# A two-layer decoder on one core: PSUM tiles of single values, value writes on ScalarE's queue, and another order of expert blocks

## The chip, the core and the metric

The kernel runs on one core of one Trainium2 chip. The metric is the device time of one execution in microseconds (us); lower is better. A core has a TensorE (PE) for matrix products, a VectorE (DVE), a ScalarE (ACT), a GpSimd (POOL) and a SyncE (SP); each runs its own instructions in order and waits for the others by semaphores. DMA transfers are issued from the queues of SP, ACT and POOL. PE writes to PSUM, which has eight banks of 128 partitions x 512 floats; the kernel's tiles lie in the on-chip SBUF, its inputs and scratch arrays in DRAM.

## The reference, cut to what matters

The function is a decoder of two layers over x (4 sequences of 512 rows, 256 wide) with a context of 4 x 1601 rows. Each step adds to x and normalizes:

```python
x = _layernorm(x + _L0_attn_ref(x, ...))            # an inner gradient step per token
x = _layernorm(x + _L0_xattn_ref(x, ctx, ctx, fside, ...))
x = _layernorm(x + _L0_ffn_ref(x, ...))             # 8 experts, the best 2 per row
x = _layernorm(x + _L1_attn_ref(x, ...))            # 16 heads, causal
x = _layernorm(x + _L1_xattn_ref(x, ctx, ctx, mask, ...))   # 16 heads, rotary
x = _layernorm(x + _L1_ffn_ref(x, ...))
```

Two parts of it bear on the change. The experts, of which each row needs only two:

```python
y = vmap(_expert_ffn)(xf, Wi, bi, Wg, bg, Wo, bo, gamma, beta)
# h = gelu(xf @ Wi + bi) * sigmoid(xf @ Wg + bg); r = xf + h @ Wo + bo; normalized, * g + b
out = einsum('te,eth->th', c, y)                    # c: the two weights of each row
```

and the values of the last cross attention, `V = value @ Wv.T` for each context. They don't depend on x, and so can be computed at any time before they are used.

## The kernel before

All products are in float32. The work goes through four stages: the first attention (to about 240 us), the first cross attention with the choice of experts (to 529 us), the experts (547 to 1001 us), and the second layer with both attentions and the last feed-forward part (1001 us to the end). Within a stage, the order of the instructions on each engine is that of the Python code (`manual_schedule`): nothing is moved by a scheduler.

**PSUM.** From the second stage on, `psum_stage` (L48) gives three pairs of banks, tag "wide" (`wide()`, L55), and two single banks, tag "bank" (`bank()`, L58), each used in turn. A tile that comes round again waits until the last reader of its former contents is done.

**Early values.** At the end of the second stage, `value(b, k)` (L782) computes the values of the contexts 2 and 3 for one block of 128 context rows: four PE records (two products of 128x256, each seen as two records), and a copy by ScalarE (L791) into an SBUF tile in the layout that the later attention needs. There are 26 of them, in the order 9 of context 2, 13 of context 3, 4 of context 2 (L831). Two successive values share one pair of banks, through the list named `halves`. The first 9 are placed between the parts of the last normalization and of the routing (`tail()`, L834 to L841); the other 17 follow `blocks_left` (L551), whose VectorE work gives the tables of the dynamic expert blocks. After the values (2, 8), (3, 12) and (2, 12), SP writes what is finished to the DRAM arrays `vd` (L793, L795, L797; 1291.5, 1865.5 and 574 KB). They are read again in the second layer's cross attention. Meanwhile POOL scatters the rows of x to the experts' array `xs` (L546).

**SP's queue at the start of the third stage.** After the writes to `vd`, SP issues the eight weight loads of the second layer (L79; the first is qkvQ), four small vectors (L92, L85), the rows of the first two expert blocks (`rows_of`, L922), and two eWo loads (L407). The weights take memory that the values' tiles had.

**Expert blocks.** `run(blocks, work)` (L1110) processes a list of blocks of 256 rows. A block of kind "f" (first) has the first 256 rows of one expert and one set of weights; a block of kind "m" (more) has two halves of 128 rows, each with a dynamically chosen expert and weights of its own. An expert's weights are eWi and eWg (1028 KB each) and eWo (1408 KB). Those of an "f" block are loaded by SP (`load_expert`, L399), those of an "m" block by POOL with indirect DMAs, and so are the rows (L922 and L928). Iteration i does, in this order: `first_half(i)` (products with eWi and eWg, gelu and sigmoid on ScalarE, the product of both on VectorE, L977; it also issues the loads of eWi and eWg of block i+1), `turned(i+1)` (transposes of the rows, L939), `second_half(i-1)` (products with eWo, VectorE's sum from L997 on, normalization, the write to `ys` by SP, L1012; for an "m" block, PE's second half waits for VectorE's first sum), `rows_of(i+2)`, the next eWo loads (three are held ahead), and one step of the side work `attention_first` (L1019). The steps of the side work go by position in the list: 0 to 2 load constants and tables, 3 to 6 fill rows of `qd` and `ksd`, 7 to 10 fill `kcd` (1601 KB each, DRAM to DRAM), 11 clears tiles on POOL, 12 to 15 each load a piece of the mask by SP (L1068), which VectorE turns into an additive row (L1072).

The order of the blocks is written out by hand as a string (L1143), 8 "f" and 11 "m".

Of the kernel before, what the change touches and what calls it, by code (L numbers as in the profile page):

```python
# [18 lines left out]
B, S, D = 4, 512, 256  # L19
S2 = 1601  # L20
NT = S // P
NKT = (S2 + P - 1) // P
# [12 lines left out]
def kn_of(kt):  # L35
    return P if kt < NKT - 1 else KLAST
# [3 lines left out]
def decoder(ctx: ExitStack, tc: tile.TileContext, a: dict, out: bass.AP):  # L40
    nc = tc.nc
# [13 lines left out]
    def wide():  # L55
        return psum["A"].tile([P, 2, 512], F32, tag="wide", name="wide")

    def bank():  # L58
        return psum["B"].tile([P, 512], F32, tag="bank", name="bank")
# [15 lines left out]
    def weight(pool, name):  # L75

        src = a[name]
        t = pool.tile([P, 2, src.shape[1]], F32, tag=name, name=name)
        nc.sync.dma_start(t, src.rearrange("(c p) n -> p c n", p=P))  # L79
        return t  # L80
# [117 lines left out]
    def mm(ps, terms):  # L198

        n = len(terms)  # L200
        for i, (l, r) in enumerate(terms):
            nc.tensor.matmul(ps, l, r, start=(i == 0), stop=(i == n - 1))  # L202
# [12 lines left out]
    with (  # L215
# [15 lines left out]
        ps = wide()  # L231
# [4 lines left out]
        ps = bank()  # L236
# [387 lines left out]
    VROW = NH * VW + HD - 1  # L624
    vd = {b: tc.dram_tile((P, NKT * VROW), F32, name=f"vd{b}") for b in (2, 3)}


    with tc.tile_pool(name="p2", bufs=2) as p2, ExitStack() as ordered:
# [7 lines left out]
        ps = wide()  # L636
# [3 lines left out]
        ps = bank()  # L640
# [3 lines left out]
        ps = wide()  # L644
# [3 lines left out]
        ps = bank()  # L648
# [115 lines left out]


        xaV = weight(p2, "xaV")
        values, places, halves = [], {}, []

        def rows_of_values(first):

# [10 lines left out]

        def value(b, k):  # L782
            kn = kn_of(k)
            if not halves or len(halves) == 2:
                halves[:] = [wide()]
            else:
                halves.append(halves[0])
            ps = halves[0][:, len(halves) - 1, :D]
            mm(ps[:kn], [(ctxTs[b][:, c, k * P : k * P + kn], xaV[:, c, :]) for c in range(2)])
            dst = places[b, k][:kn, : NH * VW].rearrange("p (h r) -> p h r", r=VW)  # L790
            nc.scalar.copy(dst[:, :, :HD], ps[:kn].rearrange("p (h r) -> p h r", r=HD))  # L791
            if (b, k) == (2, 8):
                nc.sync.dma_start(vd[2][:, : 9 * VROW], big_of(2, 0, 9))  # L793
            if (b, k) == (3, NKT - 1):
                nc.sync.dma_start(vd[3], big_of(3, 0, NKT))  # L795
            if (b, k) == (2, NKT - 1):
                nc.sync.dma_start(vd[2][:, 9 * VROW :], big_of(2, 9, NKT))  # L797

        def big_of(b, k0, k1):
            first = places[b, k0]  # L800
            return bass.AP(first.tensor, first.offset, [first.ap[0], [1, (k1 - k0) * VROW]])
# [29 lines left out]
        order = [(2, k) for k in range(9)] + [(3, k) for k in range(NKT)]  # L831
        order += [(2, k) for k in range(9, NKT)]
        values = [lambda b=b, k=k: value(b, k) for b, k in order]
        for n in (3, 0, 0, 0, 0, 0, 6, 0, 0, 0, 0, 0):  # L834
            if len(values) < len(order):
# [5 lines left out]
            values = values[n:]  # L841
# [52 lines left out]
    with tc.tile_pool(name="p3", bufs=2) as p3, ExitStack() as ordered:  # L894
# [245 lines left out]
                next(work, None)  # L1140
            second_half(blocks[-1], None, outs)

        order = "ffmfmfmmfmfmmfmfmm" + "m" * 1  # L1143
        counts = {"f": iter(range(E)), "m": iter(range(NDYN // 2))}
        blocks = [({"f": "first", "m": "more"}[k], next(counts[k])) for k in order]
        def beside():
# [25 lines left out]
    with ExitStack() as s4:  # L1172
# [148 lines left out]
        def context(b, keys, values, here=None):  # L1321
# [20 lines left out]
            for i in sorted({*keys, *values}):  # L1342
                if here is None:
                    src = lambda n=len(stream): chunk(n)
                    stream.append((b, i))
                else:
                    src = lambda i=i: here[2 * i : 2 * i + 2]
                eng = nc.gpsimd if here is None else nc.vector
                if i in keys:
                    items += [lambda s=src, i=i, c=c: key(s, i, c, eng) for c in range(2)]  # L1350
                if i in values:
                    items += [lambda s=src, k=k: value(s, k) for k in range(4 * i, min(4 * i + 4, NKT))]
# [650 lines left out]
```

## Time and profile before

| what | value |
|---|---|
| median of 3 runs | 2409.47 us (2403.08 to 2413.41) |
| the profiled execution, its own time | 2402.61 us |
| its span, first to last instruction | 2400.8 us |
| PE busy | 2275.6 us (95%) |
| DVE, ACT, POOL busy | 1239.0, 1064.2, 360.0 us (52%, 44%, 15%) |
| DMA moved | 244.14 MB, mean 102 GB/s |

By stretches of the span, as the windows of the trace give them (busy us; share of the DMA engines):

| stretch, us | length | PE | DVE | ACT | granted clock | DMA |
|---|---|---|---|---|---|---|
| 487 to 507 | 20 | 15.84 | 9.25 | 4.62 | 0.83 | 0.14 |
| 507 to 529 | 22 | 17.89 | 7.03 | 6.71 | 1.00 | 0.47 |
| 529 to 547 | 18 | 0.19 | 0.00 | 0.00 | 0.55 | 0.85 |
| 547 to 593 | 46 | 41.99 | 6.79 | 18.98 | 0.84 | 0.45 |
| 593 to 1001 | 408 | 382.45 | 157.88 | 207.26 | 0.98 | 0.76 |
| 1001 to 2401 | 1400 | 1368.33 | 885.56 | 738.44 | 0.98 | 0.15 |

A line of the timeline has the start and the length of a group of instructions in us, the engine (PEld is PE's weight load, SPq a DMA issue in SP's queue), the source line, the operation, the tile written and the tile read, the shape, the number of instructions, and in brackets the idle time of the engine just before, with what ended it. The granted clock is the share of full speed that PE's clock was allowed.

### The profile page before, as it was taken

To read this page: it belongs to the slowest core of one execution; us is meant where nothing else is said; L and a number is where in the kernel's file an instruction comes from. 1 tells how busy PE (TensorE), PEld (TensorE's weight loads), DVE (VectorE), ACT (ScalarE), POOL (GpSimd) and SP (SyncE) were. 2 spreads that over 40 slices of the span, in tenths; PEclk is the share of its full clock that TensorE was granted. 3 is DMA by queue.
4 is the path that set the end of the run, shared out by engine and by line. 5 is a ranking of instruction groups with operands and counts; after the bars stand their busy time and mean duration, and the time that the engine had idled before them with its cause. 6 is when DMAs were issued, how large, how long until landed. Compare 5 with 4: busy or idle time off the path is not lost.

```text
span 2400.8 us, 36163 instructions
## 1 busy us (share of the span) xinstructions
PE 2275.6 (95%) x14448; PEld 1289.9 (54%) x14448; DVE 1239.0 (52%) x2928; ACT 1064.2 (44%) x2103; POOL 360.0 (15%) x373
## 2 busy tenths in 40 slices
PE   7899999968999999889999999999999999999998
PEld 4767577757898988643333334333333333333266
DVE  1433234431333334356666667666766776677234
ACT  1111122213554545324555553655656566566730
POOL 1010001130122223225230010120122010000000
PEclk9999999988999999989999998999999999999999
DMA  8400311135887867341210210111110010100000
GB/s 304 173 0 1 132 55 46 45 137 178 321 333 308 338 258 300 132 147 50 67 49 27 77 64 1 37 33 59 56 58 28 25 60 15 54 11 20 30 10 27
DMA packets 77100, 244.14 MB, mean 102 GB/s; under 512 B 11640, under 2 KB 34686, under 8 KB 64638
## 3 DMA queue, kind: packets, MB, share of 16 engines
q1 hardware_dynamic: 60126, 137.41, 16.7%
q0 software_dynamic: 13632, 89.32, 9.7%
q10 hardware_dynamic: 3168, 15.03, 1.8%
q8 instruction: 116, 1.90, 0.3%
q14 instruction: 58, 0.48, 0.1%
HBM read 196.12 MB, written 56.77 MB: 105 GB/s over the span
## 4 chain that ended last, share of the span: by engine, by line
PE 50%; DVE 1%; ACT 1%; issue 0%; DVEq 0%; ACTq 0%
PE s L1458 23%; PE po L1485 12%; PE one L202 11%; PE s L202 2%; PE s L1468 1%; PE one L1443 1%; PE one L1506 1%; ACT x L171 0%; ACT ex L1472 0%; DVE pm L1415 0%; DVE one L1417 0%; PE one L1527 0%; PE one L1625 0%; PE one L1548 0%; DVE nb L166 0%
## 5 line engine op out<-in xcount | busy, mean ns | idle before, releaser
L1472 ACT ACTIVATE ex<-s 128x512 f32<-128x512 f32 (+1 forms) x1062 | 578.2, 594 | 458.2 <-PE s L1458 222.8
L1415 DVE TENSOR_REDUCE pm<-one 128x1 f32<-128x512 f32 x768 | 492.8, 685 | 159.5 <-PE s L1458 104.0
L1458 PE MATMUL s<-q,kc 32*128 32x512 f32 x1612 | 527.6, 638 | 0.8 <-ACT ex L1472 0.8
L202 PE MATMUL one<-kc,qt 32*128 32x512 f32 (+1 forms) x2048 | 482.5, 562 | 0.3 <-DVE pm L1415 0.3
L1458 PEld LDWEIGHTS s<-q,kc 32*128 32x128 f32 x1612 | 165.9, 179 | 202.5 <-issue 170.0
L1485 PE MATMUL po<-ex,v 128*32 128x256 f32 (+3 forms) x2688 | 250.9, 442 | 0.3 <-ACT ot L1498 0.3
L1417 DVE CUSTOM_DVE_ANT_0 one<-one,c_diagq 128x512 f32<-128x512 f32 x256 | 171.8, 716 | 76.0 <-PE one L202 65.1
L1485 PEld LDWEIGHTS po<-ex,v 128*32 128x32 f32 (+1 forms) x2688 | 54.1, 108 | 252.4 <-issue 244.9
L1458 PE MATMUL s<-q,ks 32*128 32x512 f32 x512 | 180.0, 650 | 5.3 <-ACT ex L1472 4.9
L202 PEld LDWEIGHTS one<-kc,qt 32*128 32x128 f32 x2048 | 164.2, 188 | 11.8 <-DVE pm L1415 7.8
L202 PE MATMUL bank<-eWo,g 128*128 128x256 f32 x608 | 141.9, 390 | 13.6 <-DVE rb L997 10.7
L202 PE MATMUL one<-ks,qt 32*128 32x512 f32 x512 | 149.7, 662 | 0.6 <-DVE pm L1417 0.6
L202 PE MATMUL wide<-xbT,eWi 128*128 128x128 f32 (+1 forms) x960 | 142.9, 310 | 4.0 <-DVE xbT L943 4.0
L202 PEld LDWEIGHTS wide<-xbT,eWi 128*128 128x128 f32 x960 | 132.9, 196 | 13.4 <-issue 3.4
L977 DVE TENSOR_TENSOR g<-g,sg 128x1024 f32<-128x1024 f32 x38 | 46.3, 1223 | 178.5 <-ACT sg L975 178.5
L202 PE MATMUL wide<-xbT,eWg 128*128 128x128 f32 (+1 forms) x960 | 137.0, 303 | 0.0
L202 PEld LDWEIGHTS bank<-eWo,g 128*128 128x128 f32 x608 | 116.4, 196 | 33.5 <-DVE rb L997 14.8
L1298 POOL TENSOR_TENSOR raw<-raw,c_cos 128x512 f32<-128x512 f32 (+1 forms) x32 | 35.0, 1094 | 654.8 <-DVE swp L1297 554.8
L202 PEld LDWEIGHTS wide<-xbT,eWg 128*128 128x128 f32 x960 | 128.1, 191 | 6.6
L1458 PEld LDWEIGHTS s<-q,ks 32*128 32x128 f32 x512 | 53.9, 185 | 83.3 <-issue 61.7
L202 PE MATMUL wide<-ctxT,q 128*128 128x512 f32 (+1 forms) x256 | 91.3, 510 | 0.8 <-DVE q L669 0.8
L975 ACT ACTIVATE g<-wide,eWi 128x128 f32<-128x128 f32 (+1 forms) x240 | 72.6, 415 | 27.0 <-PE wide L202 26.8
(326 smaller groups left out, 2943.0 us busy)
## 6 DMA issues: line engine op xcount, KB each, us to landing
xs<-zero SPq DMA_DIRECT2D x32, 512.0 KB
kc<-kcd SPq DMA_DIRECT2D x16, 800.5 KB
eWo<-in_eWo SPq DMA_DIRECT2D x8, 1408.0 KB
eWi<-in_eWi SPq DMA_DIRECT2D x8, 1028.0 KB
eWg<-in_eWg SPq DMA_DIRECT2D x8, 1028.0 KB
qt<-qd SPq DMA_DIRECT2D x32, 256.0 KB
ctxT<-in_ctxT SPq DMA_DIRECT2D x4, 1601.0 KB
kcd<-in_c_rowkc ACTq DMA_DIRECT2D x4, 1601.0 KB
```

Of the source, the lines that this page charges most:

```text
L202: nc.tensor.matmul(ps, l, r, start=(i == 0), stop=(i == n - 1))
L975: nc.scalar.activation(dst[:, k, :], pv[:, k, :], func, bias=bias)
L977: nc.vector.tensor_tensor(part, part, dst, ALU.mult)
L1298: eng.tensor_tensor(raw[:, :n], raw[:, :n], cos[:, :n], ALU.mult)
L1415: nc.vector.tensor_reduce(pm[:, t, j, c : c + 1], ps, AX.X, ALU.max)
L1417: nc.vector.tensor_tensor_reduce(out=ps, in0=ps, in1=diagq[:, 384 - t * P : 896 - t * P], scale=1.0, scalar=LOWEST, op0=ALU.add, op1=ALU.m ...
L1443: nc.tensor.transpose(pt[:, t * P : (t + 1) * P], ng.rearrange("p j r -> p (j r)"), ident)
L1458: nc.tensor.matmul(ps[:kn], kt[rows, k * P : k * P + kn], q2[rows, :], start=True, stop=cross)
L1468: nc.tensor.matmul(ps[:, k * P : (k + 1) * P], later_[:, :P], later_[:, P:], start=False, stop=True)
L1472: nc.scalar.activation(ex[:kn, h, :], ps[:kn], AF.Exp)
L1485: nc.tensor.matmul(state["po"][j * 32 : j * 32 + 32, q0:q1], (vals if cross else vself)[b % 2][:kn, k, c0 : c0 + 32], ex[:kn, j % 2, q0:q1 ...
L1506: nc.tensor.transpose(pt[:, t * P : (t + 1) * P], ot[:, t * P : (t + 1) * P], ident)
```

## The change

It has three parts. First, a value no longer shares a PSUM pair with its neighbour: of each three successive values, two take a single bank, and the third takes half of a pair of its own. Second, the three writes to `vd` are issued from ScalarE's queue instead of SP's, at the same places of the code. Third, the string that gives the order of the expert blocks is another one; the numbers of both kinds stay as they are. With positions counted from 0, "m" and "f" change places at 5 and 6, at 10 and 11, and at 15 and 16.

```diff
-        values, places, halves = [], {}, []
+        values, places, turns = [], {}, [0]
...
         def value(b, k):
             kn = kn_of(k)
-            if not halves or len(halves) == 2:
-                halves[:] = [wide()]
-            else:
-                halves.append(halves[0])
-            ps = halves[0][:, len(halves) - 1, :D]
+            turns[0] += 1
+            ps = wide()[:, 0, :D] if turns[0] % 3 == 0 else bank()[:, :D]
             mm(ps[:kn], [(ctxTs[b][:, c, k * P : k * P + kn], xaV[:, c, :]) for c in range(2)])
             dst = places[b, k][:kn, : NH * VW].rearrange("p (h r) -> p h r", r=VW)
             nc.scalar.copy(dst[:, :, :HD], ps[:kn].rearrange("p (h r) -> p h r", r=HD))
             if (b, k) == (2, 8):
-                nc.sync.dma_start(vd[2][:, : 9 * VROW], big_of(2, 0, 9))
+                nc.scalar.dma_start(vd[2][:, : 9 * VROW], big_of(2, 0, 9))
             if (b, k) == (3, NKT - 1):
-                nc.sync.dma_start(vd[3], big_of(3, 0, NKT))
+                nc.scalar.dma_start(vd[3], big_of(3, 0, NKT))
             if (b, k) == (2, NKT - 1):
-                nc.sync.dma_start(vd[2][:, 9 * VROW :], big_of(2, 9, NKT))
+                nc.scalar.dma_start(vd[2][:, 9 * VROW :], big_of(2, 9, NKT))
...
-        order = "ffmfmfmmfmfmmfmfmm" + "m" * 1
+        order = "ffmfmmfmfmmfmfmmf" + "m" * 2
```

## The prediction

> **What bounds the kernel.** The page gives PE 95% of the span. Its chain of waits carries 50% of the span by PE, but it starts at 1126 us, in the second layer's attention, where the change touches nothing; from 1001 us on PE is busy 1368 of 1400 us, so that part only shifts. What is gained or lost must therefore come from PE's own gaps before 1001 us. I read those in the timeline, from 484 to 1003 us. First the values:
>
> ```profile
> 490.25 1.99 PE L202 MATMUL wide<-xaV,ctxT 128*128 128x256 f32 x8 [2.13 <-ACT v L791]
> ...
> 517.74 1.99 PE L202 MATMUL wide<-xaV,ctxT 128*128 128x256 f32 x8 [0.46 <-ACT v L791]
> 518.91 0.37 ACT L791 COPY v<-wide 128x256 f32<-128x256 f32 x1 [1.22 <-PE wide L202]
> 519.77 0.37 ACT L791 COPY v<-wide 128x256 f32<-128x256 f32 x1 [0.49 <-PE wide L202]
> 520.20 1.99 PE L202 MATMUL wide<-xaV,ctxT 128*128 128x256 f32 x8 [0.46 <-ACT v L791]
> ...
> 529.03 0.32 SPq L797 DMA_DIRECT2D vd<-v  x1
> 531.87 0.38 SPq L79 DMA_DIRECT2D qkvQ<-in_qkvQ  x1
> ...
> 543.54 1.07 SPq L922 DMA_DIRECT2D xb<-xs  x2
> 546.81 1.08 PE L939 MATMUL bank<-ident,xb 128*128 128x128 f32 x4 [18.22 <-DMA xb<-xs]
> ```
>
> The reader is to see two limits. PE stands before every second value until ScalarE has copied the other half of the same pair: the period is 520.20 - 517.74 = 2.46 us for two values, while two copies released by PE stand 519.77 - 518.91 = 0.86 us apart, which is PE's own time for one value. And the 18.22 us gap before the first expert block is a string on SP: the last write of values at 529.03, its landing, the weights' issues from 531.87, the rows of the first blocks at 543.54. Then the expert stage, from the waits of PE between 540 and 980 us and its timeline:
>
> ```profile
> PE bank L939 <- DMA xb<-xs: 24.6, 5, 18.2
> PE bank L202 <- DVE rb L997: 10.5, 10, 3.2
> ...
> 768.01 0.63 PE L939 MATMUL bank<-ident,xb 128*128 128x128 f32 x4 [3.46 <-DMA xb<-xs]
> ...
> 858.00 0.52 DVE L1072 TENSOR_SCALAR mf<-mi 16x401 f32<-16x401 int32 x1 [12.86 <-DMA mi<-in_mask]
> ...
> 862.37 5.17 PE L202 MATMUL bank<-eWo,g 128*128 128x256 f32 x16 [3.02 <-DVE rb L997]
> ```
>
> No wait on eWi or eWg is listed: weights arrive in time. What is left is small: 24.6 - 18.2 = 6.4 us on rows of blocks, two waits of about 3 us on VectorE, which had itself waited for a piece of the mask.
>
> **Part 1: single banks.** No instruction is added; 26 values keep four PE records and one copy each. What goes is the wait inside a pair, since no tile holds two values now. A bank comes round after three values, and its copy is due 2 x 0.86 = 1.72 us after PE left it; a copy needs 0.1 + 0.37 us, and 0.4 more where a DMA issue stands before it on ScalarE, so it is covered. Were that cover gone, each value would wait the difference. In order:
> - Values 1 to 3: the transposes of x start when VectorE has x (491.35) instead of at 492.08: **0.7 us**, and the routing chain behind them shifts by it.
> - Values 4 to 9: they start at 497.6 instead of 498.29. The copies at 500.40 and 502.11 show 1.7 us per value there (granted clock 0.50 from 498 to 503 us). Two at 1.7 and four at 0.86 end at 504.5; VectorE's carry, ready at 504.8 - 0.7 = 504.1, is covered. The routing matmuls start at 504.5 instead of 507.07: **2.6 us**.
> - Values 10 to 26: the first two take banks that VectorE must read first (L525, L556). L556 stood 2.04 us after the routing matmuls (509.11 - 507.07), so value 11 starts at 506.7; 16 x 0.86 = 13.8 ends at 520.5, instead of 528.6: **8.1 us** in all, the 2.6 among it.
>
> [...] Here the granted clock fell at 497 us though no gap since 487 was over 2.13 us. [...]
>
> **Part 2: writes by ScalarE's queue.** Three issues of about 0.33 us leave SP and become three of about 0.4 us on ScalarE (its c_diagq issue took 0.39). Behind the first two stand copies, and PE behind those; part 1 covers them. The obvious hope is that SP, freed, starts its weights at once. I don't count it: the order of instructions of the changed kernel still has the qkvQ load wait for the DMA lanes that the values' writes are on, and before it waited 531.87 - 529.03 = 2.84 us for the last of them. POOL's first eWo load waits the same way (13.5 us for vd). So the string stays: last copy, last write, landing, weights (14.94 us from 531.87 to PE's 546.81), and only its start moves. The last write, issued at 521.0 instead of 529.03, comes closer to the one before it (1865 KB at the 478 GB/s of the windows from 525 to 528 us is 3.9 us): that one, issued at 517.6, has its data through at 522.3, the last (574 KB, 1.4 us) at 523.7, and qkvQ follows 0.65 us later at 524.35. Gain of parts 1 and 2 together: 531.87 - 524.35 = **7.5 us**. Bounds: 8.5 us if the two writes don't queue and the clock doesn't fall; 5 us if three more values run at half clock (3 x 0.85). The scatter of the last rows, on POOL until 519.3 before, moves 2.5 us ahead with L556 and stays covered.
>
> If the write did not hold qkvQ, up to 3.4 us more (524.35 - 521.0) would go; that is in rival C.
>
> **Part 3: order of blocks.** The same 8 whole blocks ("f") and 11 of halves ("m"), three swaps of neighbours: positions 5/6, 10/11, 15/16. The side work (tables, masks), one step per position, keeps its positions. PE's work is the same; only gaps can move.
> - *Weights of pairs.* The pair at 9, 10 stands beside the kcd copies. Before, the pair at 11, 12 stood beside two of the four, and PE ran from 797 to 833 us without a wait on weights. I take 0, bounds 0 and +6: eWg of the first half has 12.3 us from issue to use in a pair (699.1 to 711.4), and eWg landed after 13.5 us (median) in the busiest stretch, 728 to 775.
> - *Rows of whole blocks.* Six "m to f" changes before and after. SP issues the rows about 5.8 us into the block before when an f precedes that, 4.2 us after an m. Landings stood 15.2 to 15.8 us into that block in three cases, 17.9 beside kcd (f at position 10, 3.46 us). For position 11 the row gives 5.8 + 13.7 from issue to landing = 19.5, a wait of 5.2 us. [...]
> - *Mask pieces.* A piece holds VectorE when its steps fall in a fast f block behind an m: before at positions 13 and 15, 3.0 us each, and PE then ran at 5.17 instead of 3.72 us for its 16 (half clock), so 4.5 us each. After: 13 and 16 the same; 15, now an m behind an m, has its sigmoid 0.8 us later but also a reader that waits: between 0 and 4.5, taken as 2.3.
> - *End.* The last eWo half is loaded behind position 17 in both (wait of 2.92 us): 0. The activation-table load of the first block no longer waits for PE; PE ran on through it before: 0.
>
> Sum of part 3: **+2.8 us**, bounds -2 and +13.
>
> **Sum.** -7.5 + 2.8 = -4.7 us. Against the profiled execution 2402.6 - 4.7 = 2397.9 us. Its span is 2400.8; it lies 6.9 us under the median of the three runs and 0.5 us under the fastest of them (2403.1 to 2413.4), so it is an execution at the fast end. The median is what is compared: 2409.5 - 4.7 = **2404.8 us**, said as 2405.
>
> **Rivals.**
> - *B, the order costs more than the values gain.* Around positions 9 and 10 the DMA needs 4.1 MB of weights, some 2.8 MB of eWo and 3.3 MB of kcd traffic in a block of 21.6 us: 470 GB/s, where the busiest slices show 420 to 450. If the backlog passes the 12.3 us of slack, PE waits at both halves of 10 and again on the rows of 11: 6 + 6 + 4.5 of masks + half-clock starts of 1.5 each (3) = 19.5, net +12: 2421. For it: eWg's 13.5 us. Against it: the older pair beside kcd did not wait. It decides once a weight takes more than 12.3 us from issue to landing inside a pair.
> - *C, more is gained:* qkvQ isn't held by the last write (-3.4) and the new order avoids one mask stall and the rows' wait beside kcd (-4.5, -3.5): -7.5 - 11.4 = -18.9: 2391. For it: waits on shared lanes need not be on the last write. Against it: the same memory is written by the weights.
> - *D, the change doesn't do what it says:* VectorE's readers hold the two banks, so that values go on waiting and only the order acts: +2.8: 2412. Against it: only values 10 and 11 have such a reader.
>
> **Numbers.** The forecast 0.58, B 0.19, C 0.16, D 0.07. What a measurement of this kernel can tell from no change is 0.5%, 12 us: below 2397.4 or above 2421.5. The forecast's own range is 2398 to 2413 (its bounds, and about 3 us of spread of medians). Half of B is below 2421; with C's near half the range is 2394 to 2418. Faster by over 0.5%: most of C and the forecast's lower edge, 0.24. Slower by over 0.5%: most of B and a little of D, 0.16. Within: 0.60.
>
> **What would show it.** Values: PE in runs without a wait on L791, copies 0.86 us apart, the last copy near 521. SP: qkvQ near 524.4, PE's first block near 539.3; if qkvQ starts at 521, C is right there. Order: waits on rows at positions 6, 8 and 11 (the last 3 to 5 us), on VectorE at 13, 16 and perhaps 15; any PE wait on eWi or eWg speaks for B. The start of the second layer, 1001 before, should be near 996. Wrong altogether if that shift is there and the end doesn't follow it.

## The result, and the profile after

The changed kernel takes 2398.11 us (median of 20 runs, 2388.19 to 2408.62) against 2404.26 us before (20 runs beside them, 2395.72 to 2413.41). The medians lie 6.15 us apart; the ratio is 0.9966, with a 95% interval from 0.9955 to 0.9977, which is about 8 us less and under the bound of 0.5% (12 us). The forecast of -4.7 us lies close to it. The profiles show that two of its terms were wrong in opposite directions.

The profiled execution of the changed kernel took 2408.62 us and was the slowest of the 20, so its end says nothing against the medians. Its span is 2406.8 us, with PE busy 2285.7 us. Its timeline around the end of the values, with the columns as in the views of before:

```profile
515.87 0.37 ACT L788 COPY v<-wide 128x256 f32<-128x256 f32 x1 [0.49 <-PE wide L202]
516.74 0.37 ACT L788 COPY v<-bank 128x256 f32<-128x256 f32 x1 [0.49 <-issue]
518.51 0.37 ACT L788 COPY v<-bank 128x256 f32<-128x256 f32 x1 [1.40 <-PE wide L202]
520.65 0.37 ACT L788 COPY v<-wide 128x256 f32<-128x256 f32 x1 [1.76 <-PE bank L202]
523.49 0.37 ACT L788 COPY v<-bank 128x256 f32<-128x256 f32 x1 [2.46 <-remote]
...
531.84 0.33 ACTq L794 DMA_DIRECT2D vd<-v  x1
534.71 0.37 SPq L79 DMA_DIRECT2D qkvQ<-in_qkvQ  x1
546.48 1.04 SPq L919 DMA_DIRECT2D xb<-xs  x2
549.66 1.09 PE L936 MATMUL bank<-ident,xb 128*128 128x128 f32 x4 [18.26 <-DMA xb<-xs]
```

Up to 516.74 us the copies stand 0.86 us apart, as the single banks should give. Then ScalarE falters: the next three copies take 6.75 us (516.74 to 523.49) instead of 2.6, and its idle time has another releaser in each line. After that PE waits for ScalarE. So in this execution the values end no earlier than before: qkvQ starts 44.9 us after the first value's start (534.71 - 489.81), and before the change it was 44.8 us (531.87 - 487.09). SP's string behind it is the old one, with a gap of 18.26 us.

The expert stage of the same execution, from its timeline:

```profile
790.63 0.63 PE L936 MATMUL bank<-ident,xb 128*128 128x128 f32 x4 [1.62 <-DMA xb<-xs]
863.39 5.41 PE L202 MATMUL bank<-eWo,g 128*128 128x256 f32 x16 [3.16 <-DVE rb L994]
909.23 3.72 PE L202 MATMUL bank<-eWo,g 128*128 128x256 f32 x16 [0.61 <-DVE rb L994]
933.66 6.61 PE L202 MATMUL bank<-eWo,g 128*128 128x256 f32 x16 [3.00 <-DVE rb L994]
```

The "f" beside kcd waits 1.62 us for its rows, where it waited 3.46. Two mask pieces still cost PE some 3 us each, and half clock follows both (16 matmuls in 5.41 and 6.61 us instead of 3.72). Position 15 waits only 0.61 us. The waits of PE in the stage list nothing on eWi or eWg.

The next table is worked out from the timelines of all kernels that were profiled once each. "9th to last copy" is from ScalarE's copy of the ninth value to that of the last. "To first block" is from PE's start on the first value to its start on the first expert block. "Experts" is from there to the start of the second layer.

| kernel | 9th to last copy | to first block | experts |
|---|---|---|---|
| before | 21.1 | 59.7 | 454.6 |
| after | 22.0 | 59.9 | 454.1 |
| banks alone | 16.0 | 56.3 | 460.3 |
| queue alone | 21.2 | 60.3 | 453.5 |
| order alone | 21.1 | 62.2 | 448.5 |
| banks and order | 16.0 | 55.5 | 444.8 |
| banks and queue | 20.0 | 58.3 | 454.6 |
| the whole change again | 20.0 | 58.4 | 449.2 |

Outside these columns nothing changed, yet the second layer took between 1397 and 1405 us in these profiles. Before, queue alone and order alone also share one way of holding the values, pairs, yet need 59.7, 60.3 and 62.2 us to the first block. And the four profiles with the old order differ by up to 6.8 us in the experts. So a figure of a single profile is no more exact than that, and only the repeated times give the size of the whole.

### The profile page after: what moved, and what is told of

Same layout as the page of the kernel before. It is cut to its first block, busy times and chain, and to the rows that moved or that the text cites. A ratio compares the mean times of both kernels' runs of the same rounds, so it can differ in the third digit from the quotient of the medians.

```text
span 2406.8 us, 36156 instructions
## 1 busy us (share of the span) xinstructions
PE 2285.7 (95%) x14448; PEld 1295.9 (54%) x14448; DVE 1238.0 (51%) x2928; ACT 1063.1 (44%) x2103; POOL 359.6 (15%) x373
## 3 DMA queue, kind: packets, MB, share of 16 engines
q1 hardware_dynamic: 59694, 133.59, 16.2%
## 4 chain that ended last, share of the span: by engine, by line
PE 51%; DVE 1%; ACT 1%; issue 0%; DVEq 0%; ACTq 0%
PE s L1455 23%; PE po L1482 12%; PE one L202 11%; PE s L202 2%; PE s L1465 1%; PE one L1440 1%; PE one L1503 1%; ACT x L171 0%; ACT ex L1469 0%; DVE pm L1412 0%; DVE one L1414 0%; PE one L1524 0%; PE one L1622 0%; PE one L1545 0%; DVE nb L166 0%
```

## The experiments

**The three parts alone, and two of them.** Each edit is the change with the other parts left as they were before.

```diff
+            ps = wide()[:, 0, :D] if turns[0] % 3 == 0 else bank()[:, :D]   # banks
...
+                nc.scalar.dma_start(vd[...], big_of(...))                     # queue, three times
...
+        order = "ffmfmmfmfmmfmfmmf" + "m" * 2                                 # order
```

> Only the single banks; SP writes the values and the blocks keep their old order. Values theory (the gain is the removed wait inside a pair): the time falls by 6 to 9 us, ratio about 0.997; the values' copies stand 0.86 us apart, and PE's first block starts 57 us or less after the first value's start (52 to 54) instead of 59.7. If the stall of ScalarE seen in the changed kernel's profile (a copy 2.5 us late, PE 2.9 us idle, then half clock) comes from DMA issues on ScalarE's queue, it is absent here; if it is a chance event, it may be here or not. Order theory (the gain comes from the new order of blocks): ratio 1.000.

> Only the three writes on ScalarE's queue; pairs and old order. Values theory: ratio 1.000 within 0.001, the first weight load still starts about 2.8 us after the last write's issue. Queue theory (SP, freed, starts its weights sooner): the first weight load starts less than 1 us after the last copy, and the time falls by 2 to 3 us, ratio 0.999.

> Only the new order of blocks. By the forecast's term +2.8 us: ratio 1.001 (0.999 to 1.004). Order theory: 4 to 8 us faster, ratio 0.997. PE's waits: rows at positions 6, 8 and 11 of 0.7 to 5 us, VectorE with a mask piece at 13 and 16 of 3 us each, none on eWi or eWg.

> The whole change but for the queue: SP writes the values. If the queue is worth nothing, the ratio is that of the whole change, 0.9966 within 0.001. If DMA issues on ScalarE stall it, this one is 2 to 7 us faster than the whole change and has copies 0.86 us apart all through.

Measured, as ratios to before: banks alone 0.9969 (0.9960 to 0.9978), queue alone 0.9997 (0.9983 to 1.0012), order alone 0.9958 (0.9935 to 0.9981), banks and order 0.9952 (0.9936 to 0.9969). The queue is worth nothing by itself. The new order, which I took to cost 2.8 us, is faster. The gains of banks and order don't add up in the times (0.9952 instead of 0.9927), but the intervals are some 4 to 11 us wide. In the profile of banks and order the mechanism of the banks is clean:

```profile
509.30 0.37 ACT L788 COPY v<-bank 128x256 f32<-128x256 f32 x1 [0.49 <-PE bank L202]
510.17 0.37 ACT L788 COPY v<-bank 128x256 f32<-128x256 f32 x1 [0.49 <-PE bank L202]
511.03 0.37 ACT L788 COPY v<-wide 128x256 f32<-128x256 f32 x1 [0.49 <-PE wide L202]
511.89 0.37 ACT L788 COPY v<-bank 128x256 f32<-128x256 f32 x1 [0.49 <-PE bank L202]
...
518.33 0.32 SPq L794 DMA_DIRECT2D vd<-v  x1
522.54 0.38 SPq L79 DMA_DIRECT2D qkvQ<-in_qkvQ  x1
```

Every copy follows PE at 0.86 us, with no stop. The last write and qkvQ stand 4.21 us apart, where they stood 2.84 apart, since the two last writes now come 3.45 us apart instead of 4.86, which fits data that queue.

**The whole again, and without the order.**

> The whole change once more. Chance theory (the stall of ScalarE at 517 to 523 us in the first profile of the changed kernel was one execution's): no such stall, copies 0.86 us apart, PE's first block 53 to 57 us after the first value, span under 2400. Queue theory (DMA issues on ScalarE's queue delay its later work): a stall of 2 us or more among the last values again. Ratio 0.9966 within 0.001 by either.

> Banks and queue, old order. If the queue is worth nothing, the ratio is that of the banks alone, 0.997; if the queue's issues stall ScalarE once it has less slack, 0.998 to 1.000 and a stall in the profile. Waits on rows and mask as before the change: about 6 us of rows beyond the first block, two of 3 us on VectorE.

Measured: the whole 0.9969 (0.9959 to 0.9979), banks and queue 0.9980 (0.9972 to 0.9989). In both profiles ScalarE stops at the same values as in the profile after, and the values lose 4 us of the 5.2 that the banks gave (20.0 instead of 16.0 us). At this point each profile with banks and ScalarE's queue had the stop, and neither of the two with banks and SP's queue had it. That made the queue the suspect, though the two without the stop came from one chip, and these two with it from another.

**What holds qkvQ.** The second and third write are sent right after the first one, so that no write is left at the end. They carry the first nine values in place of their own, so `vd` does not get its right content in this kernel.

```diff
-            if (b, k) == (3, NKT - 1):
-                nc.scalar.dma_start(vd[3], big_of(3, 0, NKT))
-            if (b, k) == (2, NKT - 1):
-                nc.scalar.dma_start(vd[2][:, 9 * VROW :], big_of(2, 9, NKT))
+                nc.scalar.dma_start(vd[3][:, : 9 * VROW], big_of(2, 0, 9))
+                nc.scalar.dma_start(vd[3][:, 9 * VROW :], big_of(2, 0, NKT - 9))
+                nc.scalar.dma_start(vd[2][:, 9 * VROW :], big_of(2, 0, NKT - 9))
```

> The whole change, but the writes of the values of context 3 and of the last four of context 2 are issued early, behind the first write, with the nine first values of context 2 as their content (what is written to memory for these is not the values, so the output isn't the reference's). No write is under way then when the last copy ends. Hold theory (the first weight load waits for the last write to land): it starts less than 1 us after the last copy instead of 4.6 us (4.2 us after the write's issue) as with the banks alone, and PE's gap shrinks by 3 to 4 us, from 19.9 or 20.8 to about 16.5. If another thing holds the load, it still starts 3 us or more after the last copy.

Measured: the last copy at 523.52 us, qkvQ at 523.91, so 0.4 us later, instead of 3.3 us in the whole change (531.44 to 534.71). PE's gap before the first block was 16.09 us, as expected. The last write's landing holds qkvQ. With that the queue can't free SP, and rival C's part on it is out. The one run took 2397.65 us.

**Does a transfer on ScalarE stop its copies?** First, a ninth of the first write on ScalarE and all the rest on SP. Second, the first write on SP and the last two on ScalarE. Both have the banks and the order.

```diff
-                nc.scalar.dma_start(vd[2][:, : 9 * VROW], big_of(2, 0, 9))
+                nc.scalar.dma_start(vd[2][:, :VROW], big_of(2, 0, 1))            # first kernel
+                nc.sync.dma_start(vd[2][:, VROW : 9 * VROW], big_of(2, 1, 9))
...
+                nc.sync.dma_start(vd[2][:, : 9 * VROW], big_of(2, 0, 9))         # second kernel
```

> The change without the queue, except that the first of the nine values in the first write (128 rows of 287 numbers, a ninth of that write) is sent by ScalarE at the same place in its order; SP sends all the rest. [...] Theory D (data): it is the 1.3 MB of the write's data on ScalarE's queue that holds ScalarE up. Then a ninth of it costs next to nothing: values 34 to 36 us, fetch at 14 us, ratio 0.994 to 0.996.

> The whole change with the first of the three writes back on SP; the second and third stay on ScalarE. [...] Theory I (each issue from ScalarE holds up the copies behind it): the four copies behind the second write come later, values 37 us or more, ratio near 0.997.

Measured: 0.9977 (0.9961 to 0.9993) and 0.9970 (0.9960 to 0.9979). The timeline of the second kernel, which has no transfer in ScalarE's queue before 517.99 us:

```profile
508.41 0.38 ACT L788 COPY v<-wide 128x256 f32<-128x256 f32 x1 [0.49 <-PE wide L202]
509.28 0.38 ACT L788 COPY v<-bank 128x256 f32<-128x256 f32 x1 [0.49 <-issue]
511.00 0.37 ACT L788 COPY v<-bank 128x256 f32<-128x256 f32 x1 [1.35 <-PE wide L202]
513.12 0.37 ACT L788 COPY v<-wide 128x256 f32<-128x256 f32 x1 [1.75 <-PE bank L202]
515.26 0.37 ACT L788 COPY v<-bank 128x256 f32<-128x256 f32 x1 [1.77 <-remote]
```

The stop is there all the same, and ninth to last copy takes 20.0 us. Up to 509.3 us this execution and that of banks and order agree to 0.03 us in ScalarE's copies, and then they part. The first kernel's values took 40.1 us, not the 34 to 36 of theory D, and the second kernel's ratio is the one that theory I gave; but the second kernel stops some 7 us ahead of its first transfer on ScalarE. So neither such a transfer nor its data is needed for the stop, and both theories fall as its cause. (Two kernels below send no write from ScalarE at all, and have it too.)

Something else moves with the first write. The smaller of the two instruction queues that the page lists (q14) brings packets of 8 KB, one at a time (58 of them, 0.48 MB, in a run); the view doesn't say for which engine. In all fourteen profiles one comes 15 to 17 us after the first value's start. Another comes 3.6 to 3.9 us after it in the seven profiles where SP sends the first write, and 22 to 28 us after it in the seven where ScalarE does, 2 to 8 us behind the issue of that write. In the two profiles of the case it starts at 490.99 us before (3.9 us after the first value's start) and at 514.12 after (24.3). (The fetch at 14 us in the first kernel's expectation is the early one, 4 us by this count.) The second kernel has it early (near 486 us), and its stop comes at 510; the queue alone has it late (25 us after the first value's start), and no stop. So a late packet is not needed for the stop, and with pairs it does not bring one.

**A version with SP's rows ahead of the weights.** The 18.26 us gap is SP's string, and twelve loads for the second layer stand in it ahead of the first blocks' rows. Here the rows and the first eWo loads go ahead of the twelve, with the writes on ScalarE, then with the writes on SP, and then with the mask's pieces loaded one step earlier too.

```diff
-        for name in ("qkvQ", "qkvK", "xaQ", "xaK", "qkvV", "xaV", "outP", "xaO"):
-            W[name] = weight(plw, name)
+        def later_weights():
+            for name in ("qkvQ", "qkvK", "xaQ", "xaK", "qkvV", "xaV", "outP", "xaO"):
+                W[name] = weight(plw, name)
...
+            if not W:
+                later_weights()      # in run(), after the first rows and eWo loads
...
+            mi = fetched(0)          # third kernel alone; a second buffer for mi
+            yield
+            for c, (k0, kw) in enumerate(pieces):
+                nxt = fetched(c + 1) if c + 1 < len(pieces) else None
```

> The whole change, and SP issues the rows and eWo of the first expert blocks ahead of the twelve weight loads of the second layer. If the string on SP sets the gap: the rows are issued when qkvQ was, PE's gap shrinks from about 20 us to 8 or 9, the time falls by 8 to 12 us against the whole change, ratio to before 0.992. If the gap is set by what the DMA engines have to move (eWo and weights), it shrinks by 2 us at most.

> The change with the first blocks' rows and eWo asked for ahead of the twelve second-layer weights, and the three writes back on SP. If the two gains add: the values 3 to 5 us shorter than with the writes on ScalarE, so 0.988 to 0.989 (2378 to 2381 us). If the gap at the end of the values takes it back, because SP then has the last two writes ahead of the rows: 0.990 as with the writes on ScalarE.

> The run before it with the mask's pieces asked for one step before VectorE turns them. If the two stalls of about 3 us at the turned pieces are waits for the pieces' landing: 4 to 6 us less, 0.986 to 0.987. If they are VectorE's own time: 0.988 to 0.990, no better than the run before it.

Measured: 0.9902 (0.9888 to 0.9916; 2383.21 us), 0.9924 (0.9904 to 0.9944; 2386.36 us) and 0.9897 (0.9880 to 0.9913; 2379.53 us). They come from 4, 6 and 5 runs. The first is 14.9 us under the whole change measured beside it, more than the 8 to 12 expected, with a gap of 6.35 us. The timeline of the second kernel:

```profile
526.78 0.32 SPq L794 DMA_DIRECT2D vd<-v  x1
529.97 0.88 SPq L921 DMA_DIRECT2D xb<-xs  x2
...
531.88 0.43 SPq L79 DMA_DIRECT2D qkvQ<-in_qkvQ  x1
532.76 1.08 PE L938 MATMUL bank<-ident,xb 128*128 128x128 f32 x4 [6.41 <-DMA xb<-xs]
```

The rows are now the first transfer after the last write, and the gap is 6.41 us. Moving the writes to SP brought nothing on top, so the gains did not add: ScalarE's stop is in this profile too, with ninth to last copy at 19.9 us. The waits of PE in the expert stage of the third kernel, from 525 to 980 us (total, times, longest):

```profile
PE bank L938 <- DMA xb<-xs: 11.2, 5, 6.1
PE bank L202 <- DVE rb L996: 5.5, 11, 0.6
```

PE's longest wait for VectorE fell from 3.2 to 0.6 us, and VectorE turned the four pieces without waiting: the stalls were waits for the mask's pieces. The expert stage is 9.3 us shorter than in the second kernel (440.8 to 450.2), and the median 6.8 us, above the 4 to 6 expected. Part of it is the clock: 16 matmuls behind the first piece took 5.41 us in the second kernel and 3.72 in the third. The intervals of these three kernels overlap, so that the third is best of them is not shown. All three lie below both kernels of the case.

## Why the prediction was right in its sum and wrong in its parts

**Single banks: right mechanism, sizes off.** The prediction had the values' stage 8.1 us shorter. In the two profiles where nothing disturbs it, it is about 6 us (last copy 35.5 and 35.7 us after the first value's start, 41.5 before). The last 17 values gain 5.2 us, as said (8.1 - 2.6 = 5.5). The first nine gain 0.7 to 0.9 instead of 2.6 us, and the reason is the clock. The first line is of the router's products before, the second of the same products with banks alone:

```profile
494.22 0.61 PE L202 MATMUL bank<-Wr,xT 128*128 128x8 f32 x4 [1.10 <-ACT xT L196]
...
493.19 1.02 PE L202 MATMUL bank<-Wr,xT 128*128 128x8 f32 x4 [1.10 <-ACT xT L196]
```

From 493 to 497 us the granted clock was 0.96 before and 0.50 with banks alone. Half clock began 9.6 us after the first value's start before and lasted 6.83 us; with single banks it began after 5.9 to 6.6 us and lasted 10.24 us in every profile. I had taken the clock of before for the new timing. With banks alone half clock came though PE had no gap over 1.10 us since the first value's start, as before it had come with none over 2.13. Why it came sooner isn't shown. VectorE's readers held no value longer than said, so rival D is out.

**Writes queue at the end: right mechanism, too small.** I had qkvQ 3.35 us after the last write's issue (521.0 to 524.35), 0.5 us more than the 2.84 of before; it was 4.20 us, 1.4 more. With that qkvQ is 4.7 us earlier in the profile with banks alone, where I said 7.5 and gave 5 as the lower bound. Of the 4.7 us, 3.4 reach the first block, as the string from qkvQ to the first block took 1.2 us longer there (16.2 instead of 14.9 us).

**The queue.** "The obvious hope is that SP, freed, starts its weights at once. I don't count it" was right: 0.9997 alone, and qkvQ follows the last copy at once when no write is outstanding.

**The step "so it is covered" failed, though not for the reason that stood against it.** In eight of the ten profiles with single banks (that with the early writes, where it stops too, not counted) ScalarE stops, and at most 1.2 of the 5.2 us are left; in the other two all of it is. No profile with pairs shows it. The cover of 1.7 us per bank that I gave to ScalarE's copies is too little for it. Its cause is open. The runs show that neither the writes on ScalarE's queue, nor their data there, nor the late packet of the instruction queue is needed. Whether the chip matters isn't known: the two profiles without a stop come from one chip, and at least seven of the eight with it come from two others. How often executions without a profile have it isn't known either.

**Order: wrong sign.** The sum had +2.8 us. Four profiles with the old order have 453.5 to 460.3 us in the experts (mean 455.7), six with the new one and SP's old string 444.8 to 454.1 (mean 448.3): about -7.5 us. The repeated times agree in the sign. Of kernels measured side by side that differ in the order alone, the new one's median is 11.0 us lower with pairs, 3.7 with banks, and 3.3 with banks and queue, though the intervals of the last two pairs of kernels overlap.

By the windows of the stage, PE's idle time fell from a mean of 30.7 to 27.9 us, and its busy time from 425.0 to 420.4 us for the same 2612 matmuls, so over half of the 7.5 us is clock. The busy times overlap (423.4 to 427.8 us with the old order, 417.7 to 426.1 with the new), and how much of the clock's part is the order's and how much chance isn't shown. By the steps of the prediction:

- *Weights of pairs*, 0: right, no wait on eWi or eWg anywhere. Rival B is out.
- *Rows*, +0.5: measured about -2.5. Behind the first block the waits on rows sum to 6.4 to 8.5 us with the old order and 3.7 to 5.4 with the new. No run shows the term of +0.5: it had 3.5 us for the rows beside kcd, where the row gave 5.2, and the wait there is 1.5 to 2.7 us. Both were too high.
- *Mask pieces*, +2.3: position 15, which I charged, waits only 0.6 us. At the first stalled piece half clock follows in four of four profiles with the old order, and in three of six with the new; at the second, in four of four and in one of six. The second stall before, then both in the profile with the order alone:

```profile
910.03 5.23 PE L202 MATMUL bank<-eWo,g 128*128 128x256 f32 x16 [3.15 <-DVE rb L997]
...
856.57 5.41 PE L202 MATMUL bank<-eWo,g 128*128 128x256 f32 x16 [3.54 <-DVE rb L997]
...
926.42 3.72 PE L202 MATMUL bank<-eWo,g 128*128 128x256 f32 x16 [2.58 <-DVE rb L997]
```

  With the order alone, after the first stall of 3.54 us the 16 matmuls take 5.41 us, after the second of 2.58 us they take 3.72, the full clock. I had charged 4.5 us for each stalled piece; without half clock the block is only 2.1 us longer (24.0 us from its start to the next one's, where an undisturbed "f" takes 21.9).

Rival C came near in the number of its order half, one mask stall and the rows beside kcd, at -8 us. But neither wait went away; the rows' became shorter, and the second stall is 2.6 to 3.0 us instead of 3.2 to 3.4. Its other half, that qkvQ goes free, was wrong.

**The sum.** It came out near by luck, because two errors cancelled. On the way to the first block, banks and queue together brought -0.2 to 1.4 us in three profiles (the banks without the queue 3.4 and 4.2) instead of 7.5, and the order saved time instead of costing 2.8. The times measured side by side divide the whole's 8.1 us (2406.26 to 2398.14) into 4.8 for banks and queue (2401.44) and 3.3 for the order. The 4.8 and the profiles' 1.4 differ by about as much as single profiles do.

## What to carry to other kernels

When a wait on a buffer is taken away, sum the gain with the clock as it will be in the new timing, and move the last transfer's landing and the queue behind it too; a stage that ends in a string of transfers passes on less than it gains (here 3.4 of 4.7 us). Look at the string first: putting twelve loads that nobody needs yet behind the rows that PE waits for brought 12 us of gap, three times what the banks brought. And an order of blocks should be costed with every stall's aftermath, since a stall of 3 us cost 1.5 to 3 us more here where half clock followed (5.17 to 6.77 us for 16 matmuls instead of 3.72).

## What the runs showed of the hardware

- ScalarE stopped between copies although PE's values were ready (in the profile after PE was through with a value by 520.15 us, and its copy came at 523.49): three copies in 6.0 to 6.75 us instead of 2.6, in eight of ten profiles, and always behind the copy of the 16th value, about 27 us after the first value's start. In all eight, the next two steps from copy to copy are 1.4, 2.1 or 2.8 us, about two, three or four times 0.71 us (2.14 and 2.84 in the profile after). That it is always the same place speaks for the program's code rather than for chance, but two profiles pass the place without it. No run here explains it.
- With the first write in ScalarE's queue, one packet of the smaller instruction queue came 22 to 28 us after the first value's start instead of 3.6 to 3.9 (seven profiles each), behind that write's issue at 20 to 21 us.
- In the records of the granted clock before and after, the stretches of half clock lasted 3.41, 6.83, 10.24, 13.65, 20.48 and 23.89 us, but for the last one, which the end of the run cuts (4.94 and 5.00 us). At the values it was 6.83 us before and 10.24 with single banks.
- After a stall of 3.00 us half clock followed in the profile after (6.61 us for 16 matmuls), and with a ninth of the write on ScalarE the same matmuls took 3.72 us after 3.01. So the length of the stall alone did not decide it here.
- With the early writes, the four in a row on ScalarE's queue took 0.37, 0.44, 0.94 and 1.27 us to issue; in the profile after, the three single writes took 0.36, 0.33 and 0.33.
